# Three of seven product evictions moved from ScalarE copies to VectorE sums read from PSUM

## The chip, the cores and the metric

The kernel runs on one core of one Trainium2 chip. The metric is the device time of one execution in microseconds, from the start to the end of the program on that core. All arithmetic is in fp32. TensorE (PE) multiplies and writes to banks of PSUM; ScalarE (ACT), VectorE (DVE) and GpSimd (POOL) work on SBUF, and ScalarE and VectorE also read the banks. Each engine runs its instructions in the order in which they were issued.

## The reference

The input x is 8 x 1024 tokens of 512 features. It is normalized, and two things are made of the normalized rows: a gated linear recurrence over the 1024 steps of each sequence, and a mixture of experts. Their product is added to x. Cut to what matters here:

```python
xn = _layernorm(x, axis=-1)
proj = xn @ W1 + b1                           # 512 -> 3 x 1024
hidden, forget_gate, input_gate = jnp.split(proj, 3, axis=-1)
# a recurrence over the steps, in logarithms; then out = out_h @ W2 + b2
s = _L0_attn_ref(xn, ...)
shared_out = _swiglu(xn, shared_gate_w, shared_up_w, shared_down_w)   # silu(x@g) * (x@u) @ d
routed_out = ...                              # each token through one of 32 experts
x = x + s * _silu(shared_out + routed_out)
```

## The kernel before

The kernel has two phases. The first makes the recurrence and the shared expert, and sorts the tokens by expert; the second runs the 32 routed experts and writes the output. The change is in the first phase alone.

**Chunks and jobs.** The 8192 tokens are cut into 16 chunks of T = 512. For each chunk 20 jobs are run (`JOBS`): for each of four pairs of 128-feature blocks the forget gate f, the input gate i, the hidden h, and the shared expert's gate g and up projection u. A job multiplies a 512 x 256 block of weights with the chunk's 512 x 512 transposed rows (`xnT`). There are 320 jobs; the first three (NPL) are made by plain multiplication, the other 317 by Strassen's scheme in Winograd's form, with seven products P1 to P7 of half size in place of eight.

**Products and banks.** `multiply(name, n)` issues a product: two matmuls in the code, each of which the profile shows as two of 256 columns. P1, P6, P7 and P4 of a job accumulate one after the other in one bank (`b`, three of them in rotation). P5 starts a second bank (`c`) and P3 accumulates onto it; P2 has a third (`a`). The a and c banks are two in rotation (x0 and x1): P5 of the next job takes the bank that P2 left, and P2 of the next job takes the bank that P3 left. So what a bank holds must have been read before the next product writes it.

**Evictions.** After P1, P2, P5, P6, P3 and P7 ScalarE copies the bank to SBUF (tiles p1, a, p5, u2, c, u3; `evict`, line 908, and with the bias line 910). Then `join` (line 920) adds two of these copies in SBUF: a + p1 and c + u2 on VectorE, u3 + p5 on GpSimd (on VectorE in chunk 0). P4 is copied to the output tile directly. p1, a, p5, u2, c and u3 have two buffers each. In the profile the tiles p1 and p5 are both called p, u2 and u3 both u.

**The order.** The order is written out by hand (`manual_schedule`). Time is cut into slots; in each one product is issued, seven slots to a job, in the order of `ORDER`: P1 of job n, P4 of job n-2, P5 of n, P7 of n-1, P2, P6 and P3 of n. Other steps are put on slots with `at(slot, what)`, and a sum is put one slot after its product. Between the products the matmuls of the output projection (line 1191) are filled in, by their due numbers, from chunk 1 on.

**What else VectorE and ScalarE do in these slots.** A `Cell` for each pair computes the gates and the recurrence on 128 x 1024 tiles: ScalarE takes absolute values (960), exponentials (964), logarithms (968), sigmoids (983, 987) and a relu (990), with a table load at each change of function; VectorE takes a difference (972, which needs the second logarithm), two corrections (976, 980), the value (993, needs 990), a product (996) and two scans (1005). A `Hidden` multiplies the shared expert's parts (1034 to 1041). `t_sum` (814) makes the four sums of the chunk's rows. `Prep` normalizes and turns the next chunk (586 to 692; 622 are its transposes). `out_combine` (1143, on VectorE and GpSimd) and `project_out` (1203, 1214, 1180, 1209, 1210, 1217) serve the output projection; 1203 and 1214 are VectorE sums of 512 columns with one operand in a bank. In chunk 0 GpSimd and VectorE also make sums of the weights (773 to 779, 1087). At the end of the phase the dispatch (1351 to 1423) numbers the tokens by expert with small VectorE operations.

Of the kernel before, what the change touches and what calls it, by code (L numbers as in the profile page):

```python
# [11 lines left out]
ALU = mybir.AluOpType  # L12
# [22 lines left out]
def tile_kernel(  # L35
# [45 lines left out]
    nc = tc.nc  # L81
# [27 lines left out]
    def work(name):  # L109
# [11 lines left out]
        out=upper, in_=ones, pattern=[[1, P]], compare_op=ALU.is_gt, fill=0.0,  # L121
# [49 lines left out]
    class Chunk:  # L171
# [295 lines left out]
        def bias(self, t):  # L467
            if t < len(self.tiles):
                n, r = self.tiles[t][1], self.rest[t]
                nc.vector.tensor_tensor(r[:n, H : 2 * H], r[:n, H : 2 * H], b2b[:n, :], ALU.add)  # L470
# [65 lines left out]
    HT = T // 2  # L536
# [21 lines left out]
    now = 0  # L558
    steps = {}

    def at(slot, what, *args):
        assert slot >= now
        steps.setdefault(slot, []).append(lambda: what(*args))
# [194 lines left out]
    def blocks(n):  # L758
        w = natural[n]
        return [w[:, k : k + KQ, m : m + P] for m in (0, P) for k in (0, KQ)]  # L760
# [62 lines left out]
    outs, banks = {}, {}  # L823

    def out_of(n):
        c, q = divmod(n, JC)
        p, kind = JOBS[q]
        outs[n] = jp.tile([P, 2, T], FP, tag="out", name=f"{kind}{c}_{p}", bufs=7)
        return outs[n]
# [35 lines left out]
    def multiply(name, n):  # L865

        c = n // JC
        kind = JOBS[n % JC][1]
        A11, A12, A21, A22 = blocks(n)
        S = sums.get(n)  # L870
        b = xnTs[c]

        def B(k, m):
            return b[:, k * KQ : (k + 1) * KQ, m * HT : (m + 1) * HT]

        lhs, rhs, bank = {
            "P1": lambda: (A11, B(0, 0), "b"),
            "P2": lambda: (A12, B(1, 0), "a"),
            "P3": lambda: (S[:, 3], B(1, 1), "c"),
            "P4": lambda: (A22, tsum[c, 4], "b"),  # L880
            "P5": lambda: (S[:, 0], tsum[c, 1], "c"),
            "P6": lambda: (S[:, 1], tsum[c, 2], "b"),
            "P7": lambda: (S[:, 2], tsum[c, 3], "b"),
        }[name]()
        new = name in ("P1", "P2", "P5")
        if new:
            if bank == "b":
                ps = ps_b.tile([P, 512], FP, tag="b", name=f"b{n}")
            else:
                ps = ps_x.tile([P, 512], FP, tag=f"x{(n + (bank == 'a')) % 2}", name=f"{bank}{n}")  # L890
            banks[n, bank] = ps
        ps = banks[n, bank][:, :HT]
        for k in range(KQ):
            nc.tensor.matmul(  # L894
                ps, lhsT=lhs[:, k, :], rhs=rhs[:, k, :],
                start=(new and k == 0), stop=(k == KQ - 1),

                skip_group_check=True,
            )

        def part(tag, bufs):
            o = jp.tile([P, HT], FP, tag=tag, name=f"{tag}{n}", bufs=bufs)
            outs[n, tag] = o
            return o

        def evict(o, block):
            if block is None or kind in "gu":
                nc.scalar.copy(o, ps)  # L908
            else:
                nc.scalar.activation(o, ps, AF.Identity, bias=bias(n, block))  # L910

        if name == "P1":
            out_of(n)
            evict(part("p1", 2), 0)
            return
        o = outs[n]

        def join(eng, out, *tags):
            l, r = (outs.pop((n, tag)) for tag in tags)
            at(now + 1, lambda: eng.tensor_tensor(out, l, r, ALU.add))  # L920

        if name == "P2":
            evict(part("a", 2), None)
            join(nc.vector, o[:, 0, :HT], "a", "p1")
        elif name == "P5":
            evict(part("p5", 2), None)
        elif name == "P6":
            evict(part("u2", 2), 0)
        elif name == "P3":
            evict(part("c", 2), None)  # L930
            join(nc.vector, o[:, 0, HT:], "c", "u2")
        elif name == "P7":
            evict(part("u3", 2), 1)
            join(nc.gpsimd if c else nc.vector, o[:, 1, HT:], "u3", "p5")
        elif name == "P4":
            evict(o[:, 1, :HT], 1)
            natural.pop(n)
# [627 lines left out]
    for now in range(END):  # L1565
        name, back = ORDER[now % 7]
        n = now // 7 - back
        if now < 7 * NPL:
            plain(now // 7, now % 7)
        if NPL <= n < NJOB:  # L1570
            multiply(name, n)
        for step in steps.pop(now, ()):
            step()
        while filled < due(now):
            next(fill)
            filled += 1
# [105 lines left out]
    with tc.tile_pool(name="wo", bufs=3) as wo, tc.tile_pool(name="so", bufs=3) as so:  # L1682
        n = nc.values_load(  # L1683
            nov[0:1, 0:1], min_val=0, max_val=MAXOV,
            skip_runtime_bounds_check_because="a sum of at most MAXOV comparisons of counts that sum to N",
        )
# [60 lines left out]
```

## Time and profile before

| | |
|---|---|
| median of 13 timed runs | 4390.88 us (4382.13 to 4398.91) |
| the profiled execution | 4410.65 us |
| its span, from the first to the last instruction | 4408.6 us |
| busy: PE, DVE, ACT, POOL | 4179.0, 2378.9, 2148.2, 1399.6 us |
| last eviction on line 908 | starts at 2749.0 us |
| L908 copies a, c (317 each) | 117.8 and 119.7 us |
| L920 sums on GpSimd | 300 of about 0.73 us |

The page cuts the span into 40 equal slices of 110 us; each digit is a busy share in tenths, and PEclk is the clock that TensorE was granted, in tenths of full speed:

```profile
PE   7999999999999999999999999998888888888998
DVE  6655455455555554554554554255665556665632
ACT  5776676677676666766766766111112112222210
POOL 5222122122112112221221245444444444444431
PEclk9999999999999999999999999999989999999999
```

The first phase is the first 25 slices. A line of a timeline shows the start, the duration, the engine, the line of the kernel, the operation, output <- inputs, and in brackets how long the engine sat idle before it and whom it waited for. A line such as `DVE d L972 <- ACT m L968` in the list of waits reads: VectorE's instruction on line 972 waited for ScalarE's on line 968.

### The profile page before, as it was taken

Reading aid. Unit: us, or ns where it says so; the run is one execution under the profiler, and the core shown is the slowest. Engines: PE = TensorE matmul, PEld = TensorE weight load, DVE = VectorE, ACT = ScalarE, POOL = GpSimd, SP = SyncE. Lnnn points to the kernel's source line nnn. Section 1 sums busy time; section 2 is a strip of 40 time slices with the busy share of each in tenths; the row PEclk is TensorE's granted clock in tenths of the full one; section 3 lists DMA queues with packets and bytes.
Section 4 is the critical chain, followed back from the end, with each engine's and each line's share of the span. In section 5 each row is a group of like instructions: output and inputs, shape, how many; then the busy total and the mean of one; then the engine's idle time right before and its main releaser. Section 6 shows DMA issues by size and latency. Waiting matters only on the chain. (4 is left out here: it accounts for less than half of the span.)

```text
span 4408.6 us, 60006 instructions
## 1 busy us (share of the span) xinstructions
PE 4179.0 (95%) x21515; PEld 3685.0 (84%) x21515; DVE 2378.9 (54%) x3760; ACT 2148.2 (49%) x4095; POOL 1399.6 (32%) x1310
## 2 busy tenths in 40 slices
PE   7999999999999999999999999998888888888998
PEld 5788888888888888888888888777777778888898
DVE  6655455455555554554554554255665556665632
ACT  5776676677676666766766766111112112222210
POOL 5222122122112112221221245444444444444431
PEclk9999999999999999999999999999989999999999
DMA  7767566666666666676666555766566555566674
GB/s 251 235 215 235 202 214 224 215 215 215 209 223 212 208 224 212 204 232 207 213 221 217 193 187 172 240 202 194 187 195 199 194 187 197 197 214 222 223 239 157
DMA packets 567694, 926.13 MB, mean 210 GB/s; under 512 B 41469, under 2 KB 328093, under 8 KB 567394
## 3 DMA queue, kind: packets, MB, share of 16 engines
q1 hardware_dynamic: 539810, 832.29, 57.3%
q0 software_dynamic: 27584, 89.98, 6.3%
q8 instruction: 172, 2.82, 0.3%
q14 instruction: 128, 1.05, 0.1%
HBM read 805.27 MB, written 134.92 MB: 213 GB/s over the span
## 5 line engine op out<-in xcount | busy, mean ns | idle before, releaser
L894 PE MATMUL b<-t,sums 128*128 128x256 f32 x2536 | 652.9, 380 | 3.4 <-ACT u L908 1.7
L1191 PE MATMUL u<-wP,s 128*128 128x256 f32 x2032 | 596.3, 379 | 2.7 <-issue 2.7
L310 PE MATMUL acc<-e_h,e_wd 128*128 128x296 f32 (+15 forms) x2048 | 550.5, 414 | 0.4 <-issue 0.4
L894 PEld LDWEIGHTS b<-t,sums 128*128 128x128 f32 x2536 | 481.1, 190 | 71.8 <-ACT u L908 2.9
L310 PEld LDWEIGHTS acc<-e_h,e_wd 128*128 128x128 f32 x2048 | 397.2, 202 | 77.7 <-issue 7.2
L1191 PEld LDWEIGHTS u<-wP,s 128*128 128x128 f32 x2032 | 385.7, 190 | 57.0 <-issue 4.9
L894 PE MATMUL c<-xnT,sums 128*128 128x256 f32 x1268 | 326.0, 380 | 11.6 <-ACT p L908 10.3
L894 PE MATMUL c<-t,sums 128*128 128x256 f32 x1268 | 326.5, 380 | 5.9 <-ACT a L908 5.9
L894 PE MATMUL a<-xnT,nat 128*128 128x256 f32 x1268 | 326.6, 380 | 0.2
L894 PE MATMUL b<-xnT,nat 128*128 128x256 f32 x1268 | 325.4, 379 | 0.0
L894 PE MATMUL b<-t,nat 128*128 128x256 f32 x1268 | 325.4, 379 | 0.0
L259 POOL DMA_INDIRECT e_xs<-rec,fours x276 | 272.6, 988 | 94.9 <-issue 82.5
L375 PE MATMUL e_b<-e_ts,e_sm 128*128 128x148 f32 (+12 forms) x864 | 147.0, 321 | 161.3 <-issue 109.5
L894 PEld LDWEIGHTS c<-xnT,sums 128*128 128x128 f32 x1268 | 240.1, 190 | 47.0 <-issue 7.5
L894 PEld LDWEIGHTS c<-t,sums 128*128 128x128 f32 x1268 | 241.3, 190 | 39.4 <-issue 6.6
L375 PEld LDWEIGHTS e_b<-e_ts,e_sm 128*128 128x128 f32 x864 | 131.1, 219 | 166.6 <-issue 112.6
L894 PEld LDWEIGHTS a<-xnT,nat 128*128 128x128 f32 x1268 | 241.2, 190 | 34.3 <-ACT c L908 1.5
L894 PEld LDWEIGHTS b<-xnT,nat 128*128 128x128 f32 x1268 | 240.9, 190 | 33.2 <-issue 0.5
L384 ACT COPY e_s<-e_b 128x296 f32<-128x296 f32 (+12 forms) x216 | 84.6, 392 | 377.1 <-PE e_b L375 188.0
L894 PEld LDWEIGHTS b<-t,nat 128*128 128x128 f32 x1268 | 240.9, 190 | 32.7
L910 ACT ACTIVATE u<-b,vec 128x256 f32<-128x256 f32 x378 | 180.2, 477 | 178.3 <-PE b L894 175.9
L480 POOL DMA_INDIRECT out_dram<-e_rest,idx x84 | 86.0, 1024 | 494.5 <-DVE e_rest L479 469.6
(288 smaller groups left out, 8215.5 us busy)
## 6 DMA issues: line engine op xcount, KB each, us to landing
sums<-sdram SPq DMA_DIRECT2D x300, 512.0 KB
nat<-in_L_attn_W_dram SPq DMA_DIRECT2D x192, 512.0 KB
e_w<-L_ffn_routed_gate_w_dram SPq DMA_DIRECT2D x128, 512.0 KB
e_w<-n_L_ffn_routed_up_w_dram SPq DMA_DIRECT2D x128, 512.0 KB
e_wd<-L_ffn_routed_down_w_dram SPq DMA_DIRECT2D x32, 2048.0 KB
wP<-tdram SPq DMA_DIRECT2D x127, 512.0 KB
nat<-L_ffn_shared_gate_w_dram SPq DMA_DIRECT2D x64, 512.0 KB
nat<-n_L_ffn_shared_up_w_dram SPq DMA_DIRECT2D x64, 512.0 KB
```

Of the source, the lines that this page charges most:

```text
L259: nc.gpsimd.indirect_dma_start(out=r[:, b, :], out_offset=None, in_=rec1.rearrange("n (a d) -> (n a) d", a=NA), in_offset=bass.IndirectOff ...
L310: nc.tensor.matmul(accs[m][:, :W], lhsT=self.wd[:, j, m * P : (m + 1) * P], rhs=h[:, :W], start=(j == 0), stop=(j == NI - 1),)
L375: nc.tensor.matmul(ps[:, g * w : (g + 1) * w], lhsT=self.block(n, g, k, j), rhs=self.rows[n][:, k, :], start=(new and g == 0 and k == 0), ...
L384: nc.scalar.copy(o[:, :W], ps[:, :W])
L480: store = nc.gpsimd.indirect_dma_start(out=of[:, :], out_offset=bass.IndirectOffsetOnAxis(ap=col[:n, :], axis=0), in_=o, in_offset=None, b ...
L894: nc.tensor.matmul(ps, lhsT=lhs[:, k, :], rhs=rhs[:, k, :], start=(new and k == 0), stop=(k == KQ - 1),  skip_group_check=True,)
L910: nc.scalar.activation(o, ps, AF.Identity, bias=bias(n, block))
L1191: nc.tensor.matmul(ps[:, q, :], lhsT=lhs[:, q * P : (q + 1) * P], rhs=w[:, p, :],  start=(q == 0 and p == 0 and name in ("P1", "P2", "P5") ...
```

## The change

The copies a, c and u3 go. The second, third and seventh products are read by VectorE where they lie, in the bank, and added to the copy that was made earlier (p1, u2, p5); for the seventh product the bias is added in the same instruction, where there is one. All three sums run on VectorE, in all chunks, on the slot on which the sums ran before. p1 and u2 have one buffer each in place of two.

```diff
         if name == "P1":
             out_of(n)
-            evict(part("p1", 2), 0)
+            evict(part("p1", 1), 0)
             return
         o = outs[n]
 
-        def join(eng, out, *tags):
-            l, r = (outs.pop((n, tag)) for tag in tags)
-            at(now + 1, lambda: eng.tensor_tensor(out, l, r, ALU.add))
+        def join(out, tag, block=None):
+            r = outs.pop((n, tag))
+
+            def add():
+                if block is None or kind in "gu":
+                    nc.vector.tensor_tensor(out, ps, r, ALU.add)
+                else:
+                    nc.vector.scalar_tensor_tensor(out, ps, bias(n, block), r, ALU.add, ALU.add)
+
+            at(now + 1, add)
 
         if name == "P2":
-            evict(part("a", 2), None)
-            join(nc.vector, o[:, 0, :HT], "a", "p1")
+            join(o[:, 0, :HT], "p1")
         elif name == "P5":
             evict(part("p5", 2), None)
         elif name == "P6":
-            evict(part("u2", 2), 0)
+            evict(part("u2", 1), 0)
         elif name == "P3":
-            evict(part("c", 2), None)
-            join(nc.vector, o[:, 0, HT:], "c", "u2")
+            join(o[:, 0, HT:], "u2")
         elif name == "P7":
-            evict(part("u3", 2), 1)
-            join(nc.gpsimd if c else nc.vector, o[:, 1, HT:], "u3", "p5")
+            join(o[:, 1, HT:], "p5", 1)
         elif name == "P4":
             evict(o[:, 1, :HT], 1)
             natural.pop(n)
```

In the changed kernel the sums are lines 923 (plain) and 925 (with the bias), and the lines behind them are 4 higher than before.

## The prediction, made before the changed kernel had run

> **What bounds the kernel now.** I read the stretches of 200 us first, then TensorE's waits, then the timeline around single sums. The stretches (columns: busy us of each engine with its instruction count, the granted clock, the DMA share, GB/s):
>
> ```profile
> 200.00:400.00 200.00, 200.00 (x933) 175.09 (x932) 103.23 (x151) 140.35 (x249) 44.33 (x47) 1.00 0.68 221
> 1400.00:1600.00 200.00, 200.00 (x933) 175.09 (x932) 104.19 (x156) 140.36 (x249) 41.57 (x48) 1.00 0.67 216
> 2400.00:2600.00 200.00, 198.58 (x922) 171.92 (x921) 116.36 (x225) 124.76 (x230) 48.83 (x54) 1.00 0.61 198
> ```
>
> From 200 us on TensorE has no gap: 933 matmuls in 200 us, one every 214 ns, in every undisturbed stretch of the first phase. ScalarE (140 of 200) and VectorE (103 of 200) have room on average. So taking work off ScalarE buys nothing there: a gain can only come from waits that TensorE has today, and a loss from waits that it gets. The waits of the first phase stand in its start-up; this is the list of TensorE's waits from 40 to 170 us (total us, times, longest):
>
> ```profile
> PE c L894 <- ACT p L908: 10.3, 7, 2.4
> PE c L894 <- ACT a L908: 5.9, 2, 3.8
> PE b L894 <- ACT u L908: 1.7, 3, 0.9
> PE c L894 <- POOL sums L777: 1.3, 1, 1.3
> ```
>
> 19.2 us in all; behind that the first phase has only two waits on VectorE's t (1.4 us, near 2575). One of the start-up's waits has a second price:
>
> ```profile
> 89.39 2.04 PE L894 MATMUL c<-t,sums 128*128 128x256 f32 x4 [3.79 <-ACT a L908]
> 91.22 1.91 PE L894 MATMUL b<-t,sums 128*128 128x256 f32 x4
> ```
>
> Four matmuls take 1.91 us here and 1.03 elsewhere, and the granted clock from 90 to 96 us is 0.55. Some 14 matmuls come 0.427 us apart in place of 0.216: 2.9 us lost after a wait of 3.79. After waits of 2.40 and less the group takes 1.10, so no such loss.
>
> **The parts of the change.**
>
> *ScalarE loses three evictions a job*: copies a (117.8 us) and c (119.7 us), and u3 of the seventh product (189 of 474 ns and 128 of 373 ns, 137 us): 375 us in all. All of it lies beside TensorE; alone worth 0. What counts is that ScalarE reaches its other work earlier, above all the second logarithm (L968 m), for which VectorE's L972 waits 255.4 us in 61 times.
>
> *GpSimd loses 300 sums* of 0.73 us (219 us). Nothing on the path waits for them; worth 0.
>
> *VectorE gets 300 sums more* (317 jobs less the 17 whose seventh sum it made already), and all 951 read one operand from the bank. The trace has no sum of 256 from a bank, but one of 512 (L1214) beside one of 512 from memory alone (L814), in min/median/max ns:
>
> ```profile
> L814 DVE TENSOR_TENSOR t<-xnT x32: 675/681/1209, 23.0 to 2581.2; 128x512 f32<-128x512 f32 x32
> L1214 DVE TENSOR_TENSOR o<-u,a x32: 675/682/690, 241.6 to 2792.2; 128x512 f32<-128x512 f32 x32
> ```
>
> 682 against 681: a bank costs VectorE nothing extra, so I take 0.42 us, the median of the sums from memory at L920; for the biased form the same, since L976 (three operands) takes what L996 takes, 1.23 us on 1024. Below, it could be half of L1214 (0.34). Above, 0.9 is what L920 takes where GpSimd is busy; L1214's maximum of 690 says that sums from a bank escape this, L814's 1209 that others do not. [...] VectorE's busy time rises by 300 x 0.42 = 126 us less what contention gives back: far from full on average.
>
> *The bank is now held until VectorE comes to it.* This decides. A sum keeps its place in VectorE's order, one slot behind its product, but where a copy by ScalarE freed the bank and the sum could lag (two buffers each), TensorE now waits for the sum: P2's holds back P5 of the next job, P3's holds back P2 of the next job, P7's holds back P4 of its own, four slots later each. So I compared, in the trace of before, where each sum ends with where that product starts. In most jobs the sum is 2 to 4 us early. The tight one in each 20 jobs is the cell of pair 1:
>
> ```profile
> 1434.70 1.16 ACT L968 ACTIVATE m<-m,ones 128x1024 f32<-128x1024 f32 x1
> 1435.89 1.56 DVE L972 TENSOR_TENSOR d<-d,m 128x1024 f32<-128x1024 f32 x1 [2.79 <-ACT m L968]
> 1438.27 1.03 PE L894 MATMUL b<-t,nat 128*128 128x256 f32 x4
> 1439.51 0.41 DVE L920 TENSOR_TENSOR u<-a,p 128x256 f32<-128x256 f32 x1
> 1439.56 1.03 PE L894 MATMUL c<-t,sums 128*128 128x256 f32 x4
> 1442.15 1.03 PE L894 MATMUL a<-xnT,nat 128*128 128x256 f32 x4
> 1442.62 0.38 DVE L920 TENSOR_TENSOR u<-c,u 128x256 f32<-128x256 f32 x1
> ```
>
> VectorE idles 2.79 us for the logarithm, then has L972, L976, L980, two transposes and the sums back to back. P2's sum ends at 1439.92, 0.36 behind the start of P5 (1439.56); P3's at 1443.00, 0.85 behind P2's start (1442.15). With the change the logarithm comes earlier by what leaves ScalarE ahead of it: in this cell ScalarE's copy p of P1 starts at 1430.12, its product ended at 1429.37, and with the evictions u (1424.22), a (1425.54) and c (1429.87) gone it starts some 0.65 earlier; behind it one more u goes, a step of 0.26: 0.9 us. Against it stand the seventh sum that now queues behind L972 (0.42) and some 0.07 from the sum's end to the matmul. P2's sum: -0.36 + 0.9 - 0.49 = just in time. P3's: -0.85 + 0.9 - 0.49 = 0.45 late, with the slower restart (1.10 for 1.03) 0.5 us. The cells of pairs 2 and 3 are 0.3 to 0.7 late today and come out early by the same sum; at a chunk's end P2's sum is 0.58 late in every other chunk, partly from contention that a bank avoids: 0.2 on average. 15 chunks x (0.5 + 0.2) = **11 us** lost; 0 if ScalarE gains 1.4 us, 28 if it gains nothing.
>
> *The end of the phase*: the dispatch's small operations fill VectorE without a gap from 2552 to 2578:
>
> ```profile
> 2566.01 1.03 PE L894 MATMUL a<-xnT,nat 128*128 128x256 f32 x4
> 2570.76 1.03 PE L894 MATMUL c<-t,sums 128*128 128x256 f32 x4
> 2576.76 0.98 DVE L920 TENSOR_TENSOR u<-a,p 128x256 f32<-128x256 f32 x1
> ```
>
> This sum ends at 2577.74, P5 of the next job starts at 2570.76: 6.98 late. Three seventh sums join ahead of it (+1.26), the logarithm is 0.9 earlier, the sum itself loses its contention (-0.56): 6.8. The waits on t (1.4) vanish in it: 5.4. It is longer than 3.79, so the clock falls as at 90 us: +2.9. **8 us** lost (5 without the clock). [...]
>
> *The start-up* is where waits go. The p waits (10.3) come from ScalarE's cell work ahead of P5's copy; with some 0.7 us gone ahead of each of seven, 5 us go. The two waits on a (5.9) and the clock's 2.9 come from copies behind a sigmoid that waits for VectorE's L980; the sum no longer passes there. But VectorE is full between 60 and 80 and between 130 and 150 us: the sum of g at 75.47 ends 6.9 us behind the start of P5 that it will hold back, and others 2 to 6. Much of that goes, since sums there take up to 2.58 us behind GpSimd and no longer wait for copies; and ScalarE's first copy of a job, with one buffer now, waits for P2's sum. I set the new waits at 7 us: 5 + 8.8 - 7 = **7 us** gained; between 15 gained (none of the new waits) and 6 lost.
>
> Sum: -7 + 11 + 8 = +12 us. Against the profiled execution (4410.65 us; its span is 4408.6) that is 4423. The profiled one is 0.45% above the median of the 13 timed runs (4390.88), and I set the forecast against the median: **4403 us**. The second phase has no edited instruction and moves along.
>
> **Rivals.**
> - *VectorE falls behind for good in each cell* (slower, 4425 to 4440): ScalarE gains nothing before the logarithm, because its copies there wait for products anyway. Then four cells in each chunk hold TensorE: sums late by 0.36 to 0.85 today, with 0.49 on top, some 2 us a chunk: 15 x 2 + 8 - 7 = +31, with the start-up at its worse end +44. It decides from the point where L972 starts less than 0.4 us earlier than today against P4. For it: 255 us of waiting on that logarithm. Against: ScalarE runs without idle through the burst.
> - *The sums are in time and only relief is left* (faster, 4376 to 4382): GpSimd's 219 us and the copies' waits (604 us of VectorE's idling before sums, for a alone) free VectorE so that the late sums in the steady part vanish, and the start-up gains 13 to 20 of its 22 us, with the end at 5. Against: VectorE's saturated stretches.
> - *It doesn't show* (within 0.2%, 8.8 us): the start-up's gain pays for the end, and the steady part loses only a few us. This needs only one term to be off by 4 us.
>
> **How the numbers follow.** A measurement of this kernel can tell about 0.2% from no change. The forecast's case, a loss of 9 to 30 us, 0.40; VectorE falling behind 0.14; no difference 0.27; faster 0.19. So slower 0.54, same 0.27, faster 0.19. The range leaves out a tenth on each side: from the lesser gain of the start-up case (4378) to a loss of 42 us (4433).
>
> **What would show it.** In TensorE's waits a p and a of ScalarE shrink and VectorE's sums (L923, L925) appear. A wait of 5 to 7 us stands near 2570, with a slower clock behind it; the cell of pair 1 shows one of about half a us at P2 in each chunk, and the count of matmuls in 200 us falls from 933 to about 928. L972 starts about 0.9 us earlier against P4. The sums of 256 take 0.42 us with no doubled ones. Wrong would be: 933 kept (the sums are in time), a p wait that grows (ScalarE held by its single buffers), or a change in the second phase.

## The result, and the profile after

The changed kernel takes 4442.43 us (median of 12 runs, 4414.70 to 4446.75), the kernel before 4394.57 us (54 runs, 4382.13 to 4409.66): 48 us more. The ratio of the means is 1.0098 [1.0086, 1.0109], 43 us. The forecast was 4403 us, the range ended at 4433. The profiled execution of the changed kernel took 4421.57 us, near the short end of its runs; so what it shows is less than what the median lost.

The page of after, busy time by engine and the slices of 110 us:

```profile
PE 4183.8 (95%) x21515; PEld 3680.8 (83%) x21515; DVE 2396.0 (54%) x4060; ACT 1854.2 (42%) x3144; POOL 1110.1 (25%) x1010
...
PE   7999999999999999999999999999888888988998
...
DVE  6655555455555554554554544256556566665642
ACT  5565565465565555655655545122112112222210
POOL 6200011001001001000100034434444445444431
PEclk9999999999999999999999999999999999999999
```

The work has moved as the diff says: 951 copies leave ScalarE (2148.2 us to 1854.2), 300 sums leave GpSimd (1399.6 to 1110.1), and VectorE, with 300 instructions more, is busy only 17 us more than before. Nothing here shows a loss. The stretches of 200 us of after (busy us and count of PE, PEld, DVE, ACT, POOL; granted clock; DMA share; GB/s) do:

```profile
200.00:400.00 200.00, 200.00 (x933) 174.93 (x932) 104.18 (x172) 119.16 (x179) 18.63 (x23) 1.00 0.68 219
1400.00:1600.00 200.00, 199.93 (x930) 174.48 (x929) 104.72 (x178) 118.67 (x178) 18.61 (x23) 1.00 0.67 214
2400.00:2600.00 200.00, 195.28 (x895) 168.26 (x894) 117.13 (x243) 101.00 (x157) 32.87 (x35) 0.98 0.60 196
2600.00:2800.00 200.00, 191.80 (x870) 166.20 (x868) 85.27 (x134) 96.52 (x146) 80.03 (x81) 0.98 0.56 177
```

The steady part keeps 930 to 933 matmuls. The last two rows lose: 895 where before had 922, and 870 where before's row of the same stretch is this:

```profile
2600.00:2800.00 200.00, 197.34 (x914) 172.38 (x913) 88.11 (x115) 112.91 (x197) 108.32 (x109) 1.00 0.64 210
```

TensorE's waits in after from 2500 to 2850 us (total us, times, longest); from 185 to 2500 us the list is empty:

```profile
PE b L894 <- issue: 5.5, 2, 4.8
PE u L1195 <- issue: 3.2, 1, 3.2
PE c L894 <- DVE u L923: 2.7, 2, 2.3
PE b L894 <- DVE g L923: 2.4, 1, 2.4
...
```

The two waits on VectorE's sums are the ones that were foretold for the end of the phase. The largest entry names no engine at all ("issue": the engine waited for nothing that the profile shows). Here is its place in the timeline of after (weight loads and sums that don't matter here left out):

```profile
2598.76 1.03 PE L894 MATMUL b<-t,nat 128*128 128x256 f32 x4
...
2604.46 1.52 POOL L1442 DMA_INDIRECT tab<-tok,cell  x1 [0.30 <-issue]
...
2607.54 0.95 POOL L1442 DMA_INDIRECT tab<-tok,cell  x1 [0.30 <-issue]
2609.42 0.47 ACT L910 ACTIVATE p<-b,vec 128x256 f32<-128x256 f32 x1 [8.77 <-remote]
2609.95 2.07 PE L894 MATMUL b<-t,sums 128*128 128x256 f32 x4 [4.79 <-issue]
...
2611.03 0.48 DVE L925 SCALAR_TENSOR_TENSOR i<-b,vec,p 128x256 f32<-128x256 f32 x1 [5.17 <-remote]
```

ScalarE, TensorE and VectorE stand for 5 to 9 us although the profile has the products that they need as long done, and then all go on within 2 us. What GpSimd does meanwhile is the row of L1442: the scatters of the token table (L1438 in before), which it has issued one after the other, most of them 1.26 us apart, since 2585. When the row ends, the others go on; the group behind takes 2.07 us for 1.03, and the granted clock from 2600 to 2620 is 0.83. In before GpSimd's sums (L920), each waiting for its job, stood between these scatters:

```profile
2601.54 0.73 POOL L920 TENSOR_TENSOR h<-u,p 128x256 f32<-128x256 f32 x1 [4.24 <-ACT u L910]
2602.43 0.98 POOL L1438 DMA_INDIRECT tab<-tok,cell  x1 [0.16 <-issue]
...
2606.24 0.96 POOL L1438 DMA_INDIRECT tab<-tok,cell  x1 [0.30 <-issue]
2611.94 0.72 POOL L920 TENSOR_TENSOR f<-u,p 128x256 f32<-128x256 f32 x1 [4.74 <-ACT u L910]
2612.82 0.98 POOL L1438 DMA_INDIRECT tab<-tok,cell  x1 [0.16 <-issue]
```

The trace has them there in rows of 4 at most, in after in rows of 18, 13 and 13 (a row: indirect DMAs with no other instruction of GpSimd between them, whose starts are at most 2.2 us apart).

What the others stood for can be read one step further, since the trace also keeps the time of each increment of a semaphore, the signal by which one engine tells the others that it is done. ScalarE starts at 2609.42, 0.02 us behind an increment by TensorE at 2609.40; four more follow at 2610.85, 2610.93, 2611.00 and 2611.08. Counted from the end, as the profile models it, of the last matmul that raises this semaphore, these five come 4.7 to 6.4 us late; the median of the run is 0.014 us. So it is TensorE's signals that come late and in a burst; ScalarE's and VectorE's own never come 0.5 us late, the end of the program left out.

To place the losses I counted, in each trace, when TensorE starts its 650th, 11700th, 11800th and 12900th matmul. The stretches between are the start-up, the steady part, the planning of the token table (near 2575 us) and the last chunk with the scatters. In us:

| kernel | to 650 | to 11700 | to 11800 | to 12900 |
|---|---|---|---|---|
| before | 186.0 | 2374.6 | 23.5 | 252.1 |
| after | 188.7 | 2376.5 | 29.0 | 267.0 |
| after, second profile (after_again) | 189.7 | 2376.1 | 28.8 | 280.3 |

So +3, +2, +5.5 and +15 in one execution, and +4, +1.5, +5 and +28 in another. The steady part, on which the forecast dwelt longest, is the smallest term, and the last chunk, which it left out, the largest.

### The profile page after: what moved, and what is told of

Read it like the earlier page. It is cut to its first block, busy times and chain, and to the rows that moved or that the text cites. A ratio compares the mean times of both kernels' runs of the same rounds, so it can differ in the third digit from the quotient of the medians.

```text
span 4419.6 us, 58928 instructions
## 1 busy us (share of the span) xinstructions
PE 4183.8 (95%) x21515; PEld 3680.8 (83%) x21515; DVE 2396.0 (54%) x4060; ACT 1854.2 (42%) x3144; POOL 1110.1 (25%) x1010
## 5 line engine op out<-in xcount | busy, mean ns | idle before, releaser
L1147 POOL TENSOR_TENSOR s<-h 128x256 f32<-128x256 f32 x128 | 106.1, 854 | 1355.3 <-ACT f L910 996.1
L259 POOL DMA_INDIRECT e_xs<-rec,fours x276 | 274.2, 993 | 94.0 <-issue 82.2
L976 DVE TENSOR_TENSOR d<-d,m 128x1024 f32<-128x1024 f32 x64 | 80.8, 1263 | 303.1 <-ACT m L972 296.8
L910 ACT ACTIVATE p<-b,vec 128x256 f32<-128x256 f32 x189 | 89.6, 474 | 366.9 <-PE b L894 188.0
```

The lines of the kernel that those rows point to most:

```text
L259: nc.gpsimd.indirect_dma_start(out=r[:, b, :], out_offset=None, in_=rec1.rearrange("n (a d) -> (n a) d", a=NA), in_offset=bass.IndirectOff ...
L976: nc.vector.tensor_tensor(d, d, self.li, ALU.subtract)
L1147: eng.tensor_tensor(o, l, r, op_)
```

## The experiments

Theory G (GpSimd, "row theory"): a long row of indirect DMAs that GpSimd issues back to back holds up the other engines, and the removed sums had broken these rows. Rival V: VectorE's sums, now read from the bank, come too late. Each kernel is set against the kernel before on the same chip. The groups of runs were made apart from each other; the time of before in each is given.

**First group (before: 4367.92 us).** *p7_old*: after, the seventh product again copied by ScalarE and summed on GpSimd.

```diff
-            join(o[:, 1, HT:], "p5", 1)
+            evict(part("u3", 2), 1)
+            l, r = outs.pop((n, "u3")), outs.pop((n, "p5"))
+            eng = nc.gpsimd if c else nc.vector
+            at(now + 1, lambda: eng.tensor_tensor(o[:, 1, HT:], l, r, ALU.add))
```

> The changed kernel with the seventh product as before: copied by ScalarE, summed on GpSimd; the second and third sums from the bank stay. Theory V (sums late on VectorE, as predicted): two of the three bank sums stay, so most of the loss stays, 25 to 40 us over before. Theory G (the loss comes with GpSimd: its sums, which waited for each job, held the 64 scatters of the dispatch apart; without them the scatters run back to back and TensorE, ScalarE and SP stall beside them): within 10 us of before.

*p7_only*: the reverse, before with only the seventh sum from the bank on VectorE.

> The kernel before with the seventh product alone taken from the bank by VectorE. Theory V: 0 to 10 us over before, since the late sums are the second's and third's. Theory G: 25 to 45 us over before, nearly the whole loss.

*last_chunk_dve*: before with one word changed. No bank is read, no copy goes; only GpSimd's waiting sums leave the last chunk.

```diff
-            join(nc.gpsimd if c else nc.vector, o[:, 1, HT:], "u3", "p5")
+            join(nc.gpsimd if 0 < c < NCHUNK - 1 else nc.vector, o[:, 1, HT:], "u3", "p5")
```

> The kernel before, with one edit: in the last chunk the seventh sum runs on VectorE, from the copy in memory, and not on GpSimd. No bank is held longer and no eviction changes. Theory V: 0 to 3 us over before. Theory G: 20 to 45 us over before, and the scatters L1438 stand 1.25 us apart in long rows with stalls of TensorE beside them.

*paced*: after, with p7_old's edit in the last chunk alone.

> The changed kernel, but in the last chunk the seventh product is copied by ScalarE and summed on GpSimd as before, so that GpSimd waits for each job between its scatters. Theory V: the loss stays but for what 20 seventh sums add at the end, 30 to 45 us over before. Theory G: 5 to 15 us over before (the start-up and the late sums near 2577 remain).

| kernel | ratio | us | to 650 | to 11700 | to 11800 | to 12900 |
|---|---|---|---|---|---|---|
| p7_old | 1.0055 [1.0037, 1.0073] | +23 | 192.7 | 2382.3 | 29.7 | 253.5 |
| p7_only | 1.0076 [1.0057, 1.0095] | +31 | 193.7 | 2374.6 | 27.8 | 273.8 |
| last_chunk_dve | 1.0056 [1.0039, 1.0074] | +23 | 184.4 | 2374.6 | 23.4 | 265.5 |
| paced | 1.0023 [1.0011, 1.0035] | +11 | 191.0 | 2376.4 | 29.3 | 255.6 |

G foretold three of the four. last_chunk_dve, which has nothing of the change but GpSimd's silence in one chunk, has the last chunk's loss; paced, which has nearly all of the change, has not. p7_old missed G's price (within 10): it has no loss in the last chunk, but 7 us at the start, 6 at the planning, and 7.7 in the steady part, where ScalarE keeps one copy more and VectorE's sums are late in each chunk. That is V's mechanism, at 7.7 of the 25 us and more that V gave it; its total comes near V's by the two other terms.

**Second group (before: 4173.61 us).** *spaced*: after, with a pause of GpSimd that waits for no job.

```diff
         def enter(self, i):
             nc.gpsimd.indirect_dma_start(
...
             )
+            if i % 3 == 2:
+                for _ in range(3):
+                    nc.gpsimd.tensor_tensor(pause, pause, pause, ALU.subtract)
```

> The changed kernel, with three small sums of GpSimd on a tile of its own (about 2 us) after every third scatter of the token table; these wait for no product. Row theory (many indirect DMAs of GpSimd back to back delay the other engines, and the removed sums broke the rows): no waits of TensorE at 2600 to 2720 us, ratio to the kernel before 1.000 to 1.004. Rival (GpSimd must be held back by the jobs; a pause alone does nothing, or the scatters come too early): the waits stay, 1.007 to 1.012.

*one_row*: last_chunk_dve, with `at(first, d.enter, i)` for `at(first + (21 * i) // 10, d.enter, i)`.

> The kernel before, the last chunk's seventh sums on VectorE from memory (as in the run with that one edit) and all 64 scatters given to GpSimd at one slot: one row of some 80 us in place of rows of 12, 13 and 12. Row theory, if a row delays the other engines for as long as it lasts beyond the first dozen: 40 to 80 us slower than the kernel before, 1.009 to 1.018. Rival (each row costs one wait of 5 to 8 us, however long): 1.000 to 1.004.

*rows_apart*: before, with the pause of spaced after every third gather or scatter of the second phase.

> The kernel before, first phase untouched; in the second phase three small sums of GpSimd on a tile of its own after every third indirect DMA (gathers and the scatter of the output). Row theory: in the profile of before TensorE stands 29 times, 171 us in all, at the end of rows of 10 to 14 such DMAs; most of it goes, 60 to 150 us faster, ratio 0.965 to 0.987. Rival (these waits are for weights, sums or transfers, and the rows only lie beside them): 0.997 to 1.004.

*middle_only*: the new sums only where `0 < c < NCHUNK - 1`, else copies, sums and buffers of before.

> The new sums in chunks 1 to 14 alone; chunks 0 and 15 have the copies and the sums from memory of the kernel before. Row theory (the steady part is worth nothing, the loss sits in chunk 15 and a little in chunk 0): 0.9995 to 1.002. Rival, the prediction's term of 0.7 us in each of these chunks (10 us) and the slower sums it stood for: 1.002 to 1.004.

| kernel | ratio | us | to 650 | to 11700 | to 11800 | to 12900 |
|---|---|---|---|---|---|---|
| spaced | 1.0036 [1.0022, 1.0050] | +15 | 189.1 | 2376.2 | 29.3 | 253.5 |
| one_row | 1.0190 [1.0176, 1.0204] | +80 | 186.6 | 2374.6 | 23.0 | 331.0 |
| rows_apart | 1.0652 [1.0637, 1.0666] | +273 | 184.2 | 2374.6 | 23.4 | 254.6 |
| middle_only | 1.0030 [1.0017, 1.0042] | +13 | 188.1 | 2376.3 | 29.3 | 253.5 |

This group ran in another condition: it has the kernel before at 4173.61 us, some 200 less than the others, and its second phase shows why. (Expectations further on speak of two kinds of chips. The record numbers the chips of the five groups 8, 15, 12, 13 and 15: the second and the fifth bear the same number, with before at 4173.61 us in one and at 4396.00 in the other. So the number does not tell the two conditions apart, and what does is not shown.) TensorE's waits in the second phase, first in before (the trace that the prediction read), then in middle_only (this group), whose second phase is the same code:

```profile
PE e_b L375 <- issue: 111.4, 16, 9.8
PE e_b L375 <- ACT e_s L384: 54.1, 12, 10.6
...
```

```profile
PE e_b L375 <- DVE e_low L406: 9.4, 8, 1.7
```

In before nearly every one of these waits falls on a row of gathers (L259, L269) and scatters (L480) of GpSimd. Counted in the trace: 25 of its 26 rows of 12 to 15 overlap a wait of TensorE of over 1.5 us (165 us in all). In middle_only none of the 28 rows of 11 to 15 does. So in this condition long rows delay nobody, and this group cannot test G in the first phase; spaced says nothing on it here.

one_row seems to fit G's price exactly, and does so for another reason. Its last chunk, in the timeline:

```profile
2658.12 0.95 POOL L1438 DMA_INDIRECT tab<-tok,cell  x1 [0.31 <-issue]
...
2659.78 0.73 POOL L920 TENSOR_TENSOR u<-u,p 128x256 f32<-128x256 f32 x1
2660.54 0.37 ACT L908 COPY p<-c 128x256 f32<-128x256 f32 x1 [79.02 <-POOL u L920]
```

Here the releaser has a name. A sum of the chunk before, still on GpSimd, stood behind the 64 scatters, and ScalarE's copy needed the buffer that it reads. That is queueing in order on GpSimd, not the stall of after.

rows_apart fell the wrong way for both theories. Its waits in the second phase:

```profile
DVE e_sm L232 <- POOL e_w L230: 311.6, 26, 14.7
...
PE e_b L386 <- DVE e_low L417: 219.0, 30, 10.9
```

The pauses push GpSimd's sums of the next weights (L230) back, VectorE waits for them in order, and the sum that TensorE needs (L417) stands behind that. In this condition there was nothing to win by them either.

middle_only costs 13 us where the theory said 8 at most: the planning (5.8) lies beside the sums of chunk 14, which I had counted to chunk 15.

**Third group (before: 4368.48 us).** *after_again* is the changed kernel; *last_again* is last_chunk_dve; *until_13* has the new sums where `0 < c < NCHUNK - 2`.

> The changed kernel once more, beside the three others. The runs so far came from chips of two kinds: on one the second phase shows TensorE waiting at the end of nearly every row of 10 to 14 indirect DMAs (the profile of before, 29 waits, 171 us), on the other the same rows stand beside none (7 waits, 14 us, in the run with the new sums in chunks 1 to 14 alone). Row theory: on the first kind 1.008 to 1.012, with 8 to 15 us of waits at 2590 to 2720; on the second kind no waits there and 1.003 to 1.005, the start, the steady part and the end of the phase alone (4 + 2 + 7 us). Rival (the rows cost the same on every chip, the loss of the second phase is something else): 1.008 to 1.012 on both.

> The kernel before with the last chunk's seventh sums on VectorE, once more. Row theory: 1.004 to 1.007 on a chip whose second phase shows the waits at the rows, 0.999 to 1.0015 on one whose second phase shows none. Rival (the rows cost the same on every chip): 1.004 to 1.007 on both.

> The new sums in chunks 1 to 13 alone, so that neither the start, nor the planning of the token table (2564 to 2581 us), nor the scatters run beside them. If the accounts are right (start 4, steady 2, planning 6 to 8, last chunk the rest): 0.9995 to 1.001 on every chip, and no wait of TensorE from 185 to 2590 us beyond the 1.3 of before. Rival, the prediction's 0.7 us in each chunk: 1.002 to 1.003.

*rows_split* leaves the first phase of before alone. In the second it gives the same indirect DMAs to GpSimd at other points, without a pause:

```diff
-                    for t in range(CT):
-                        between[5 + t].append(lambda t=t: chunks[e + 2].gather_tile(t))
-            between[3 if e == E - 1 else 6].insert(0, chunk.gather_rest)
+                    between[4].append(lambda: chunks[e + 2].gather_tile(0))
+                    between[6].append(lambda: chunks[e + 2].gather_tile(1))
+                if e:
+                    between[1].append(lambda: ahead.gather_tile(2))
+            if e == E - 1:
+                between[3].insert(0, chunk.gather_rest)
+            else:
+                between[3].insert(0, lambda: chunk.gather_rest(0, 2))
+                between[6].insert(0, lambda: chunk.gather_rest(2))
```

(`gather_rest(first, last)` gathers the tiles from first to last.)

> The kernel before, the first phase untouched; in the second the same indirect DMAs are given to GpSimd at other points (two gathers of the rest at the fourth step, four gathers of rows right behind the sums of the next weights, the last gathers one expert later), so that rows of 14 become rows of 8 or fewer, and the sums of weights stand no later than before. Row theory, on a chip whose second phase shows the waits at the rows: most of 171 us goes, ratio 0.965 to 0.99; on one that shows none: 0.998 to 1.002. Rival (those waits have another cause): 0.998 to 1.004 on both.

| kernel | ratio | us | to 650 | to 11700 | to 11800 | to 12900 |
|---|---|---|---|---|---|---|
| after_again | 1.0104 [1.0085, 1.0123] | +47 | 189.7 | 2376.1 | 28.8 | 280.3 |
| last_again | 1.0052 [1.0035, 1.0070] | +26 | 186.0 | 2374.6 | 23.5 | 272.5 |
| until_13 | 1.0021 [1.0007, 1.0035] | +11 | 185.2 | 2376.1 | 23.3 | 255.2 |
| rows_split | 0.9581 [0.9564, 0.9598] | -180 | 188.8 | 2374.6 | 23.5 | 251.9 |

rows_split settles that the waits of the second phase come with the rows: with the same instructions, in a group that shows the waits, 180 us go. No row there is longer than 7 now (before: 26 rows of 12 to 15), and TensorE's waits in the second phase are these:

```profile
PE e_b L376 <- DVE e_low L407: 14.8, 14, 3.0
PE e_b L376 <- issue: 0.7, 2, 0.4
```

That is about what middle_only shows in the condition that has no such waits, and the time is near its time too (4188.81 and 4186.56 us). The edit moves the DMAs and shortens their rows in one, so for the second phase alone the length is argued, not shown; the first phase tests it in the fourth group. rows_split was not run in the condition without waits.

after_again gives a second look at the stall, in waits of other engines from 2575 to 2720 us:

```profile
ACT u L910 <- issue: 19.8, 1, 19.8
...
DVE f L925 <- remote: 8.4, 1, 8.4
...
PE b L894 <- ACT u L910: 6.4, 1, 6.4
...
```

ScalarE stood for 19.8 us beside a row of 26 indirect DMAs, without a releaser, until 2696.80, 0.08 us behind an increment by TensorE at 2696.72 that came 5.8 us late; TensorE's wait behind it is then put down to ScalarE. So the word "issue" at one engine and a named neighbour at the next can be one event.

until_13 measured 11 us where the accounts said 0 to 4: its profile has 3.6 us up to the 12900th matmul. The low end of its interval (3 us) would fit; what the rest is stays open.

**Fourth group (before: 4388.37 us).** *spaced_again* is spaced, in a group that shows the waits. *tick* is after, and in the last chunk GpSimd adds one column of each job's fourth product to itself, which makes it wait for the job.

```diff
             evict(o[:, 1, :HT], 1)
+            if c == NCHUNK - 1:
+                nc.gpsimd.tensor_tensor(tick, o[:, 1, 0:1], o[:, 1, 0:1], ALU.add)
```

*split_new* is after with the edit of rows_split, *split_new_spaced* that with the pauses of spaced.

> The changed kernel with about 2 us of GpSimd's own sums after every third scatter, once more, beside three others. Row theory: whatever the chip, no waits of TensorE at 2590 to 2720 us, and 1.002 to 1.005 (start, steady part, planning); on a chip whose second phase shows waits at the rows, that is 0.5 to 0.8 per cent less than the changed kernel. Rival (GpSimd has to wait for the jobs): 1.008 to 1.012 on such a chip.

> The changed kernel; in the last chunk GpSimd adds one column of each job's fourth product to itself, into a tile that nobody reads, so that it waits for each job as the seventh sums made it wait, with next to no work. Row theory: rows of scatters as short as before, 1.002 to 1.005. Rival (what was lost is GpSimd's part of the work, and VectorE's extra 0.4 us a job is what is late): 1.008 to 1.012 on a chip whose second phase shows waits at the rows.

> The changed kernel with the second phase's indirect DMAs in rows of 7 or fewer, as in the run with only that edit. Row theory: the second phase's waits go (on a chip that has them 0.958, as in that run), the first phase's rows of scatters stay: 0.965 to 0.969 there. Rival (with the second phase mended the change costs nothing, its loss was an interplay of the two): 0.957 to 0.960 there. On a chip without such waits: 1.003 to 1.007, the change alone.

> Both mended: the changed kernel with the second phase's indirect DMAs in short rows, and about 2 us of GpSimd's own sums after every third scatter. Row theory: 0.960 to 0.963 on a chip whose second phase shows waits at the rows, still above the run with the old sums (0.958), by start, steady part and planning (13 us). Rival (VectorE's sums are a gain once no row stands in the way): at or under 0.957 there.

| kernel | ratio | us | to 650 | to 11700 | to 11800 | to 12900 |
|---|---|---|---|---|---|---|
| spaced_again | 1.0043 [1.0027, 1.0060] | +20 | 188.0 | 2376.2 | 29.4 | 251.3 |
| tick | 1.0049 [1.0029, 1.0069] | +25 | 188.9 | 2376.3 | 29.4 | 253.7 |
| split_new | 0.9649 [0.9624, 0.9674] | -155 | 191.5 | 2376.5 | 28.8 | 277.2 |
| split_new_spaced | 0.9589 [0.9564, 0.9613] | -180 | 189.8 | 2376.6 | 28.9 | 255.3 |

Both ways of breaking the rows take the last chunk's loss away, a pause without any wait and a wait without any work. So neither the waiting itself nor GpSimd's share of the work is what matters; the rows of scatters are 5 long at most in both, 26 in split_new. split_new against split_new_spaced prices the scatters' rows alone: 25 us. Of spaced_again's 20 us the counts show some 9, of tick's 25 some 12; the rest is not placed.

**Fifth group (before: 4396.00 us).** rows_split and split_new_spaced once more, side by side.

> The kernel before with the second phase's indirect DMAs in short rows, beside the same with the new sums, on one chip: their two times are compared directly. Row theory: no long row is left in either, so this one, with the old sums, is the faster by the accounts of the start (4), the steady part (2) and the planning (7): 10 to 16 us. Rival (with the rows gone the new sums bring something): this one equal or slower.

> The same second phase, with the new sums and the pauses between the scatters. Row theory: 10 to 16 us slower than the kernel beside it, 0.2 to 0.4 per cent. Rival: equal or faster.

| kernel | ratio | median us | to 650 | to 11700 | to 11800 | to 12900 |
|---|---|---|---|---|---|---|
| rows_split_b | 0.9530 [0.9515, 0.9544] | 4189.58 | 184.1 | 2374.6 | 23.4 | 252.2 |
| split_new_spaced_b | 0.9568 [0.9552, 0.9584] | 4206.30 | 189.2 | 2376.2 | 29.3 | 253.7 |

With no long row left anywhere the new sums cost 17 us, of which the counts show 14 (5 + 1.6 + 5.9 + 1.5). The best kernel of the groups that show the waits is rows_split, with the old sums.

## Why the prediction was wrong

**The step that failed** is "*GpSimd loses 300 sums* of 0.73 us (219 us). Nothing on the path waits for them; worth 0." Nothing waits for them, but they made GpSimd wait: each held the scatters queued behind it until a job was done. Without them GpSimd ran ahead and issued its scatters in rows of 11 to 26, and beside these the other engines stood. That step was read only from who waits for the sum. The other half, what is queued behind the sum on its engine, was asked for VectorE and ScalarE and not for GpSimd. Its price: 15 to 28 us in the profiles of after, 25 us between split_new and split_new_spaced, 23 to 26 us in last_chunk_dve and last_again, where it stands alone.

**The start-up** (priced at 7 us gained, measured 3 lost: the seven starts with old sums in chunk 0 and chunk 1 have a median of 186.0 us to the 650th matmul, 184.1 to 188.8, the nine with after's start 189.2, 188.0 to 191.5). The waits of after from 40 to 185 us:

```profile
PE a L894 <- DVE i L923: 6.0, 3, 2.5
PE c L894 <- ACT p L908: 4.1, 3, 2.2
PE c L894 <- DVE g L923: 2.4, 1, 2.4
PE c L894 <- DVE u L923: 2.0, 2, 1.6
PE b L894 <- DVE h L925: 2.0, 1, 2.0
PE c L894 <- DVE wid L147: 1.5, 1, 1.5
PE a L894 <- DVE u L923: 1.3, 1, 1.3
...
```

The relief was sized right: the p waits fell from 10.3 to 4.1 us, those on a went. The new waits on VectorE's sums were set at 7 us and are 16 (13.7 in the rows above and 2.3 in shorter ones); this is the term of the start-up that failed. The clock's 2.9 us did not go either: the half clock now follows a wait of 2.37 at 71.39 us and one of 2.47 at 133.85 (granted 0.50 from 72 to 76 us and 0.57 from 134 to 138; the groups behind the two waits take 2.04 and 1.73 us for 1.03). So the prediction's reading, that waits of 2.40 and less cost no clock, does not hold.

**The steady part** (11 lost, measured 1.7): the mechanism was right and the size was not; the term that was too large is the lateness of P3's sum and of the sums at a chunk's end, 0.7 us a chunk. In the same cell of the same chunk the logarithm's sum, now L976, starts 0.9 us earlier against P4, as foretold. P2's sum ends 0.3 us ahead of P5, where the forecast had it just in time; P3's ends at 1445.73, and the product that needs it starts 0.05 behind:

```profile
1438.35 1.22 DVE L976 TENSOR_TENSOR d<-d,m 128x1024 f32<-128x1024 f32 x1 [1.90 <-ACT m L972]
...
1441.66 1.03 PE L894 MATMUL b<-t,nat 128*128 128x256 f32 x4
...
1442.22 0.43 DVE L923 TENSOR_TENSOR u<-a,p 128x256 f32<-128x256 f32 x1
...
1442.96 1.03 PE L894 MATMUL c<-t,sums 128*128 128x256 f32 x4
...
1445.32 0.41 DVE L923 TENSOR_TENSOR u<-c,u 128x256 f32<-128x256 f32 x1
...
1445.78 1.13 PE L894 MATMUL a<-xnT,nat 128*128 128x256 f32 x4
```

The last group takes 1.13 for 1.03 and starts some 0.2 late, where the forecast had 0.45. The logarithm's sum itself takes 1.22 us here and took 1.56 before, which the forecast's sum leaves out. Over all it is 0.1 us a chunk. p7_old, whose ScalarE keeps the third copy, lost 7.7 us here: about the 0.5 us a chunk that the forecast gave to this cell. That suggests that the third copy's leaving was worth more than the 0.26 us put down for it; no run tests this alone.

**The planning** (8 lost, measured 5.5 to 5.9) is right in place and kind. Its two waits, in the timeline of after:

```profile
2577.00 1.13 PE L894 MATMUL b<-t,nat 128*128 128x256 f32 x4 [2.39 <-DVE g L923]
...
2580.46 2.07 PE L894 MATMUL c<-t,sums 128*128 128x256 f32 x4 [2.33 <-DVE u L923]
```

They are two short waits in place of one of 6.8, and the clock falls behind the second (0.50 from 2580 to 2584). In before the group behind a wait of 2.40 took 1.10. Neither of these two is longer than that by itself, and together they are 4.7 us of idling in 5.8. No run here shows what rule fits both.

**The sums** took what was foretold: 0.41 to 0.43 us at L923 and never more than 0.44, where L920 from memory had means of 0.43 to 0.60; with a bias 0.48, not 0.42.

The three priced terms together measure +10.7 us in the kernels with short rows (3.2 + 1.7 + 5.8), with 1.6 for the last chunk 12.3, and split_new_spaced_b measured 17 directly. So the forecast's sum of 12 was near what it priced, but by luck: the start-up was 10 us worse than set down, the steady part 9 and the planning 2 better. What it left out is one term of 15 to 28 us. The rival whose number fits best (VectorE falls behind, 4425 to 4440) is not what happened. In after the counts show 25 us in the profiled execution and 39 in the second one, of 48 and 47 in the medians; the profiled executions were shorter than the medians by 21 and 4. These accounts end at the 12900th matmul. The stretch behind it takes 1528 to 1572 us in the eleven profiles that show the second phase's waits, 1572 in before and 1558 in after. So the totals of single executions cannot be set against the counts, and some of the loss is not placed.

## What to carry to other kernels

An instruction that nothing waits for may still be what paces its engine: before pricing its removal at nothing, look at what is queued behind it and ask how fast that would run if it were free. Waits that the profile gives to nobody ("issue", "remote") and that several engines share belong side by side with what the remaining engine is doing; here the trace of before already showed TensorE waiting over 1.5 us 28 times in the second phase, 26 of them beside a row of GpSimd's indirect DMAs. Interleave such DMAs with other work of GpSimd where that work is not late, or move them to other points, as in rows_split (180 us less); a pause costs where GpSimd's next sums are on the path (rows_apart, 273 us more).

## What the runs showed of the hardware

- Rows of indirect DMAs issued back to back by GpSimd (one each 1.26 us) stood beside idle TensorE, VectorE and ScalarE in every group but the second and the fifth, whose two kernels have no long row: in before 25 of 26 rows of 12 to 15 overlap a wait of TensorE of over 1.5 us; in rows_split and rows_split_b, with 121 rows of up to 7 each, there are four and five such waits, none over 3.1 us, 8.3 and 10.2 us in all. In the second group 28 rows of 11 to 15 had none, nor had one_row's row of 64 a late signal beside it. What separates the two conditions is not shown: chip 15 was recorded in both.
- What comes late beside these rows is TensorE's increments. I counted those over 1 us behind the modelled end of the last matmul that raises the semaphore. From 200 to 2575 us no run has one. From 2575 to 2765 us, beside the scatters, after has 6, after_again 15, last_chunk_dve 10, last_again 9, p7_only 14 and split_new 11, and the fourteen others, whose last chunk lost nothing to such a stall, have none. From 2860 us on, the end of the program left out, before has 91, rows_split 15 and the second group's four kernels none. Whether TensorE ended late or only told of it late, and why rows of indirect DMAs do this, is not shown: the ends are modelled.
- The second phase's low clock in before (0.91 to 0.95 by stretches) went with the waits: rows_split, where they are gone, was granted 0.996 over its span, before 0.975.
